# Keeping the first attention group in source order on SyncE and TensorE, and asking for its bulk loads behind the turned probabilities

## The chip, the cores and the metric

One core of one Trainium2 chip runs the whole program. The metric is the device time of one execution in microseconds (us), as the median of several executions. All arithmetic is in float32.

## The reference, cut to what matters

The program is one cross-attention layer and one gated feed-forward layer on 8 sequences of 128 tokens with 512 features, each behind a layer norm and each with its residual. In the attention there are 32 heads of 128 features:

```python
q = rmsnorm(hidden, ln_weight) @ w_q.T        # 8 x 128 x (32*128)
k, v = ctx @ w_k.T, ctx @ w_v.T
score = einsum('bqhd,bkhd->bhqk', q, k) + position_bias
score = softmax(where(mask, score, -inf)); score = where(mask, score, 0)
attn  = einsum('bhqk,bkhd->bqhd', score, v)
x = x + hidden + attn @ w_out.T               # then the gated feed-forward layer
```

## The kernel before

**Tiles and stages.** The 32 heads are handled in eight groups of four (`g` = 0 to 7, `GH` = 4, 512 features wide). All queries are projected first and stored to DRAM (`queries`). Then the attention loop (L1008) runs over the groups, and within a group over the eight sequences `b` (L1030). While the attention of group g runs, the keys and values of group g+1 are projected in the gaps; these projections use two levels of Strassen's seven products, so they consist of many short matmul steps with an addition (VectorE) or a copy (ScalarE) out of PSUM after each. The profile calls their PSUM tiles `mm_k`, `mm_v` (outer products), `m_v` (one outer product carried out as seven inner steps, on only two PSUM banks in turn) and `i_v`, `i_k` (the other inner steps).

**One sequence of a group.** `probabilities` (L547) adds mask and bias on GpSimd (`s<-pb,mneg`), lets TensorE make the four heads' scores (`sc<-k,q`), adds them to `s` on VectorE, takes the row maxima (`nmx`), and on ScalarE takes the exponentials and scales them. `transpose_p` (L582) then turns the probabilities: a VectorE transposition within 32x32 blocks (`tt<-s`), a store to DRAM (`turned<-tt`, 256 KB) and a load in another block order (`pT<-turned`, 256 KB). Both transfers are issued by SyncE, and the load waits until the store has landed. Three sequences later `attend` (L596) multiplies with the values (`av<-pT,v`; in group 0 the values are `v_back`), ScalarE copies the result out (`aT<-av`) and stores it from its own queue (`att<-aT`). Below, "pT(4)" is the turned tile of sequence 4 of group 0, "sc(1,0)" the scores of group 1, sequence 0, and so on.

**What sets the order.** A planner places the instructions of each engine, SyncE's DMA issues among them, from its own estimate of when each can run; it may let one run ahead of what stands before it in the source. `InOrder` (L49) takes that freedom away: an instruction issued through it is pinned behind the instruction that was traced before it on the same engine. Pinned instructions carry the line L60 in the profile, or that of a helper. Each engine then carries out its stream in order, so an instruction that waits holds up what stands behind it.

In group 0 the projection matmuls (`kv_tensor`) are pinned to the end of the group, while the attention's own matmuls (`tensor`: scores and `av`) are pinned for the sequences 0 to 3 only. SyncE's transfers in the loop are not pinned: `load_bias` (L811), `load_kv` (L131), `load_queries` (L816) and the two transfers of `transpose_p`. In the source, the bias of the next group and the weights `wk`, `wv` of the group after it are asked for at the start of each group, and a pair of sequences' queries (512 KB) at every even `b`, two pairs ahead.

**How much projection goes between two sequences** is counted in units: the generator `later_kv` (L644) yields a weight for each step that it issued, and the loop takes steps `while done < due(g, b)` (L992). In group 0 this gives, in source order, after the scores of sequence 6 and `av` of sequence 3: one `mm_v` product and three `m_v` steps; after the scores of sequence 7 and `av` of sequence 4: the other four `m_v` steps and two `i_v` parts.

Of the kernel before, what the change touches and what calls it, by code (L numbers as in the profile page):

```python
# [18 lines left out]
BS = 32  # L19
# [45 lines left out]
def xattn_ffn_kernel(  # L65
# [19 lines left out]
    nc = tc.nc  # L85
# [5 lines left out]
    GH = 4  # L91
# [34 lines left out]
    def load_w(name, src, eng=nc.sync):  # L126
        t = wpool.tile([P, DC, GW], F32, tag="w", name=name)
        eng.dma_start(t, src.rearrange("(c p) n -> p c n", p=P))
        return t

    def load_kv(g):  # L131
        cols = bass.ts(g, GW)
        return load_w(f"wk{g}", wkT[:, cols]), load_w(f"wv{g}", wvT[:, cols])

    def load_q(g):
        return load_w(f"wq{g}", wqT[:, bass.ts(g, GW)], sync)
# [24 lines left out]
    kv_w = {0: (wk0, wv0)}  # L161
    x_in = [acts.tile([P, 2, D], F32, tag="a", name=f"x_{i}") for i in range(B // 2)]
    for b in range(B):
        nc.sync.dma_start(x_in[b // 2][:, b % 2, :], x[b])

    vector, gpsimd, scalar, sync = (
        InOrder(tc, e) for e in (nc.vector, nc.gpsimd, nc.scalar, nc.sync)
    )
# [98 lines left out]
    def turn(eng, sync, name, src, *parts, tags=("tt", 2)):  # L267


        tag, bufs = tags  # L270
        tt = work.tile([P, 4, 4, BS], F32, tag=tag, name=f"tt_{name}", bufs=bufs)
        eng.transpose(tt, src.rearrange("q h j r -> q j h r"))  # L272
        d = next(turns)
        sync.dma_start(
            d.rearrange("i r j n -> (i r) (j n)"), tt.rearrange("p j h c -> p (j h c)")
        )
        def back():
            for to, tiles in parts:
                sync.dma_start(
                    to.rearrange("p i h c -> p i (h c)"),  # L280
                    d[:, :, :, tiles].rearrange("i r j n -> (r j) i n"),
                )
        return back
# [295 lines left out]
        return s  # L579


    def transpose_p(g, b, p):  # L582
        n = f"{g}_{b}"
        pT = work.tile([P, 4, GH, BS], F32, tag="pT", name=f"pT_{n}", bufs=4)
        turn(
            vector, nc.sync, n, p.rearrange("q h (j r) -> q h j r", r=BS), (pT, slice(None))
        )()
        return pT

# [18 lines left out]
    tensor = kv_tensor = nc.tensor  # L608
    pend = []
# [116 lines left out]
    kv_tensor = InOrder(tc, nc.tensor)  # L726
# [46 lines left out]
    for n, _ in enumerate(first_kv()):  # L773
        if n in moments_at:
            pair[moments_at[n]] = norm1_moments(moments_at[n])
        if n in scales_at:
            b = scales_at[n]
# [6 lines left out]
        if n in turns_at:  # L784
            b = turns_at[n]
# [18 lines left out]
    scalar = nc.scalar  # L804
# [3 lines left out]
    vector.tensor_scalar(rs1, mv1[:, :, 1], 1.0, EPS, ALU.mult, ALU.add)  # L808
    InOrder(tc, nc.scalar).activation(rs1, rs1, AF.Sqrt)

    def load_bias(g):  # L811
        pb = work.tile([P, GH, S], F32, tag="pb", name=f"pb{g}")
        nc.sync.dma_start(pb, pbias[g * GH : (g + 1) * GH].rearrange("h q k -> q h k"))
        return pb

    def load_queries(g, i, eng=nc.sync):  # L816
        q = acts.tile([P, GH, 2 * S], F32, tag="a", name=f"q_{g}_{i}")
        eng.dma_start(q, queries[g][:, :, bass.ts(i, 2 * S)])
        return q
# [5 lines left out]
    v = kvs[0][1]  # L825
# [12 lines left out]
    for g in range(NG):  # L838
# [13 lines left out]
        w, heads, name = rows_now, [], f"q{g}"  # L852
# [44 lines left out]
    biases, ahead = {0: load_bias(0)}, {}  # L897
# [8 lines left out]
    gpsimd, vector, kv_tensor = nc.gpsimd, nc.vector, nc.tensor  # L906
# [100 lines left out]
    todo = [(g, i) for g in range(NG) for i in range(B // 2)]  # L1007
    for g in range(NG):  # L1008
        kT, v = kvs.pop(g)
        pb = biases.pop(g)  # L1010
        if g + 1 < NG:
            biases[g + 1] = load_bias(g + 1)
        if g + 2 < NG:
            kv_w[g + 2] = load_kv(g + 2)
        if g == 0:

            ctx_later = Later()
            products = later_kv()
        if g == NG - 2:
            wo_later = Later()  # L1020
            load_wo(2)(wo_later)
        if g == NG - 1:
            tensor, vector = InOrder(tc, nc.tensor), InOrder(tc, nc.vector)
            fetched, next_fetched = {}, {}
            gpsimd, sync, wo_sums = InOrder(tc, nc.gpsimd), InOrder(tc, nc.sync), None
            biased = [masked_bias(gpsimd, g, k, pb) for k in range(2)]

            bulk = InOrder(tc, nc.scalar)
            come[1, 0] = load_att(1, 0, bulk)
        for b in range(B):  # L1030
            if (g, b) == (NG - 2, B - 1):
                come = {(0, 0): load_att(0, 0, nc.sync)}
            if b % 2 == 0:
                qT = ahead.pop((g, b // 2))
                at = todo.index((g, b // 2)) + 2
                if at < len(todo):
                    ahead[todo[at]] = load_queries(*todo[at], nc.sync if g + 1 < NG else bulk)

            if (g, b) == (0, 0):
                tensor = kv_tensor = InOrder(tc, nc.tensor)  # L1040
                vector, scalar, gpsimd = (
                    InOrder(tc, e) for e in (nc.vector, nc.scalar, nc.gpsimd)
                )
                done = next(products) + next(products)
            if g == NG - 1:


                if b + 2 < B:
                    biased.append(masked_bias(gpsimd, g, b + 2, pb))
                for _ in range(2):  # L1050
                    wo_later.next(gpsimd)
                if wo_sums:
                    wo_sums = wo_sums(gpsimd)

                def between():
                    if b == 0:
                        next(products)
                    fetched[b] = att_sums(b, 0, come.pop((b, 0)), vector)

                p = probabilities(g, b, qT, kT, pb, between, biased.pop(0))  # L1060
            elif g == 0 and b < 4:
                def one():
                    nonlocal done
                    done += next(products)

                def one_and_sum():
                    ctx_later.next(vector)
                    one()

                if b == 0:  # L1070
                    biased = [masked_bias(gpsimd, g, k, pb) for k in range(2)]
                biased.append(masked_bias(gpsimd, g, b + 2, pb))
                p = probabilities(g, b, qT, kT, pb, one_and_sum, biased.pop(0), one)
            elif g == 0 and b < 6:
                def three_sums():
                    for _ in range(3):
                        ctx_later.next(vector)

                p = probabilities(g, b, qT, kT, pb, three_sums, biased.pop(0))
            else:  # L1080
                p = probabilities(g, b, qT, kT, pb)
                for _ in range(2):
                    ctx_later.next(vector)
                if g == NG - 2:
                    for _ in range((0, 1, 1, 1, 1, 2, 2, 2)[b]):
                        wo_later.next(InOrder(tc, nc.gpsimd))
            pend.append((g, b, transpose_p(g, b, p), v))
            advance(3)

            if g == NG - 1:  # L1090
                while next(products, None):
                    pass
            else:
                while done < due(g, b):
                    done += next(products)
            if (g, b) == (NG - 2, 2):

                sums.close()
                wos = pools(outp)("wosA", 2, side="right", reuse_waits="tile")
                load_wo(0)(wo_later)  # L1100
                load_wo(1)(wo_later)
            if (g, b) == (0, 3):
                tensor, vector, scalar = nc.tensor, nc.vector, nc.scalar
            if (g, b) == (0, B - 1):
                kv_tensor = nc.tensor
            if (g, b) == (1, B - 1):
                gpsimd = nc.gpsimd
            if g == NG - 1:
                if b == 0:
                    proj.close()  # L1110
                    wos = pools(outp)("wosB", 2, reuse_waits="tile")

                    first_banks = [
                        pl.tile([P, 2, HW], F32, tag=tag, name=f"m{k}_0")
                        for k, (pl, tag) in enumerate(2 * [(ps_mm, "mm")] + 2 * [(ps_b, "i")])
                    ]
                    first_out = out_products(0, list(range(NG)), first_banks, fetched)
                n = (b + 2) % B, (b + 2) // B
                come[n] = load_att(*n, bulk)
                if b < NG - 3:  # L1120
                    wo_sums = load_wo(b + 3)
                if b:
                    next(first_out)
                if b + 2 >= B:
                    next_fetched[n[0]] = att_sums(*n, come.pop(n), gpsimd)


    scalar = InOrder(tc, nc.scalar)
# [15 lines left out]
    vector, gpsimd = nc.vector, nc.gpsimd  # L1144
# [78 lines left out]
    scalar = nc.scalar  # L1223
    for i in range(1, B // 2):
# [10 lines left out]
        tensor = nc.tensor  # L1235
# [105 lines left out]
    vector, t3 = InOrder(tc, nc.vector), h2[0, 1]  # L1341
# [227 lines left out]
    for b in range(HB):  # L1569
# [5 lines left out]
        sa, vector = coming[0], nc.vector  # L1575
# [43 lines left out]
```

## Time and profile before

| | |
|---|---|
| median of 3 runs | 1056.53 us (1056.42 to 1056.57) |
| the profiled execution: its own time | 1060.24 us |
| its span, first to last instruction | 1058.4 us |
| mean granted TensorE clock | 0.998 of full speed |
| TensorE matmuls busy | 1048.6 us (99%) |
| VectorE, GpSimd, ScalarE busy | 723.0, 558.6, 380.7 us |
| moved by DMA | 166.11 MB, 157 GB/s on average |

All start times below are microseconds from the start of the profiled execution's span. Group 0 of the attention begins at about 227 us and the last projection step that is counted to it ends at about 285 us; the products with the values of its last sequences follow by 299 us. A float32 matmul is recorded as two instructions, so "x8" for `sc` or `av` is the four heads of one sequence. An idle time is shown in square brackets with what ended it. A DMA issue is shown with the time that SyncE spent on it; how long the transfer took to land is another view.

### The profile page before, as it was taken

To read this page: it belongs to the slowest core of one execution; us is meant where nothing else is said; L and a number is where in the kernel's file an instruction comes from. 1 tells how busy PE (TensorE), PEld (TensorE's weight loads), DVE (VectorE), ACT (ScalarE), POOL (GpSimd) and SP (SyncE) were. 2 spreads that over 40 slices of the span, in tenths; PEclk is the share of its full clock that TensorE was granted. 3 is DMA by queue.
4 is the path that set the end of the run, shared out by engine and by line. 5 is a ranking of instruction groups with operands and counts; after the bars stand their busy time and mean duration, and the time that the engine had idled before them with its cause. 6 is when DMAs were issued, how large, how long until landed. Compare 5 with 4: busy or idle time off the path is not lost.

```text
span 1058.4 us, 15313 instructions
## 1 busy us (share of the span) xinstructions
PE 1048.6 (99%) x5288; PEld 859.0 (81%) x5288; DVE 723.0 (68%) x1407; ACT 380.7 (36%) x1146; POOL 558.6 (53%) x647
## 2 busy tenths in 40 slices
PE   9999999999899999999999999999999999999998
PEld 5658888876789898988889779998888865667887
DVE  4698888885577777777777645664544247889852
ACT  2541112027555656556555555531000012333100
POOL 6649776808657666656662275570000336997010
PEclk9999999999999999999999999999999999999999
DMA  8443453495555654655656567773442622120011
GB/s 283 149 170 139 155 184 120 147 359 194 176 177 179 191 184 157 208 179 182 199 170 206 179 217 233 237 277 120 164 139 67 196 99 60 41 60 0 1 40 41
DMA packets 125854, 166.11 MB, mean 157 GB/s; under 512 B 15728, under 2 KB 77424, under 8 KB 125776
## 3 DMA queue, kind: packets, MB, share of 16 engines
q1 hardware_dynamic: 111360, 133.92, 38.5%
q10 hardware_dynamic: 12544, 24.38, 6.6%
q0 software_dynamic: 1872, 6.82, 2.1%
q8 instruction: 42, 0.69, 0.3%
q14 instruction: 36, 0.29, 0.1%
HBM read 106.90 MB, written 58.20 MB: 156 GB/s over the span
## 4 chain that ended last, share of the span: by engine, by line
PE 93%; DMA 3%; POOL 2%; DVE 1%; ACT 1%; issue 1%; SPq 0%; ACTq 0%; DVEq 0%; POOLq 0%
PE i_q L60 9%; PE m L967 9%; PE m L60 8%; PE i_v L437 7%; PE d L1525 6%; PE i L1390 6%; PE i_k L404 6%; PE mm_v L522 6%; PE mm_k L501 6%; PE mm_f L1430 5%; PE mm_q L60 4%; PE av L600 4%; PE sc L555 4%; PE mm_k L60 2%; PE mm_v L60 2%; PE m_v L437 2%
## 5 line engine op out<-in xcount | busy, mean ns | idle before, releaser
L60 DVE TENSOR_TENSOR q<-q,i_q 128x512 f32<-128x512 f32 x168 | 94.6, 596 | 20.2 <-PE i_q L60 17.7
L568 ACT ACTIVATE s<-s,nmx 128x128 f32<-128x128 f32 x240 | 93.3, 390 | 28.2 <-DVE nmx L563 20.7
L399 DVE TENSOR_TENSOR v<-v,i_v 128x256 f32<-128x256 f32 (+1 forms) x150 | 76.5, 521 | 33.6 <-PE i_v L437 29.2
L540 POOL TENSOR_TENSOR s<-pb,mneg 128x512 f32<-128x512 f32 x40 | 61.4, 1536 | 66.0 <-DVE tt L272 66.0
L578 ACT ACTIVATE s<-s,ri 128x128 f32<-128x128 f32 x240 | 76.7, 390 | 43.3 <-DVE ri L576 32.1
L399 DVE TENSOR_TENSOR k<-k,i_k 128x512 f32<-128x512 f32 (+1 forms) x105 | 59.3, 587 | 26.2 <-PE i_k L404 25.9
L605 ACT COPY aT<-av 128x512 f32<-128x512 f32 x60 | 35.1, 586 | 114.2 <-PE av L600 98.9
L60 POOL TENSOR_TENSOR s<-pb,mneg 128x512 f32<-128x512 f32 x24 | 36.7, 1535 | 52.7 <-DVE tt L60 36.0
L555 PEld LDWEIGHTS sc<-k,q 128*128 128x128 f32 x416 | 53.9, 192 | 7.0 <-issue 5.3
L555 PE MATMUL sc<-k,q 128*128 128x128 f32 x416 | 55.6, 275 | 0.0
L1164 POOL TENSOR_TENSOR x<-x,u 128x256 f32<-128x256 f32 x4 | 3.0, 754 | 90.9 <-DVE x L1163 90.9
L60 PE MATMUL m<-wo,a 128*128 128x256 f32 x200 | 48.5, 380 | 0.5 <-DMA a<-att 0.5
L967 PE MATMUL m<-wo,a 128*128 128x256 f32 x200 | 48.4, 379 | 0.0
L272 DVE STREAM_TRANSPOSE tt<-s 128x512 f32<-128x512 f32 x52 | 36.8, 709 | 16.3 <-ACT s L578 15.9
L300 DVE TENSOR_TENSOR S_a<-a 128x256 f32<-128x256 f32 x22 | 10.1, 461 | 54.9 <-DMA a<-att 33.3
L600 PE MATMUL av<-pT,v 128*128 128x128 f32 x360 | 47.6, 275 | 0.0
L568 ACT ACTIVATION_READ_ACCUMULATOR s<-s,nmx 128x1 f32 x240 | 44.9, 187 | 0.0
L559 DVE TENSOR_TENSOR s<-sc,s 128x512 f32<-128x512 f32 x52 | 35.3, 679 | 12.5 <-PE sc L555 12.4
L600 PEld LDWEIGHTS av<-pT,v 128*128 128x128 f32 x360 | 43.8, 192 | 0.0
L967 PEld LDWEIGHTS m<-wo,a 128*128 128x128 f32 x200 | 38.0, 190 | 5.2
L60 PEld LDWEIGHTS m<-wo,a 128*128 128x128 f32 x200 | 37.2, 190 | 5.5 <-DMA a<-att 0.9
L60 DVE TENSOR_TENSOR gate<-gate,i 128x512 f32<-128x512 f32 (+1 forms) x60 | 32.9, 592 | 5.3 <-PE i L1390 4.6
(489 smaller groups left out, 2824.9 us busy)
## 6 DMA issues: line engine op xcount, KB each, us to landing
queries<-q SPq DMA_DIRECT2D x32, 512.0 KB, 3.8
turned<-tt SPq DMA_DIRECT2D x64, 256.0 KB, 2.8
pT<-turned SPq DMA_DIRECT2D x64, 256.0 KB, 3.1
att<-aT ACTq DMA_DIRECT2D x64, 256.0 KB, 3.0
q<-queries SPq DMA_DIRECT2D x30, 512.0 KB, 5.1
a<-att SPq DMA_DIRECT2D x23, 512.0 KB, 4.1
wq<-in_wqT_dram SPq DMA_DIRECT2D x8, 1024.0 KB, 6.6
wk<-in_wkT_dram SPq DMA_DIRECT2D x7, 1024.0 KB, 6.1
```

Of the source, the lines that this page charges most:

```text
L60: return self.tc.keep_in_program_order(getattr(self.engine, op)(*args, **kw))
L399: vector.tensor_tensor(to, *(base or [to]), out, ADD)
L404: kv_tensor.matmul(out, a[n][i], b[n][i], start=first, stop=True, skip_group_check=True)
L437: kv_tensor.matmul(out[:, bass.ts(k, S)], b[n][i][:, bass.ts(k, S)], a[n][i], start=first and k == 0, stop=True, skip_group_check=True,)
L501: kv_tensor.matmul(out, w[i][:, c, bass.ts(t, P)], src[i][:, c, :], start=(first and c == 0), stop=(c == HC - 1), skip_group_check=True,)
L522: kv_tensor.matmul(out[:, bass.ts(k, HW)], src[i][:, c, bass.ts(2 * t + k, S)], w[i][:, c, :], start=(first and k == 0 and c == 0), stop=( ...
L555: tensor.matmul(sc[:, j, :], qT[:, j, bass.ts(b % 2, S)], kT[j][:, cols], start=True, stop=True)
L568: scalar.activation(s[:, j, :], s[:, j, :], AF.Exp, bias=nmx[:, j : j + 1], accum_out=sm[:, j : j + 1],)
L578: scalar.mul(s[:, j, :], s[:, j, :], ri[:, j : j + 1])
L600: tensor.matmul(av[:, j, :], v[b // 2][:, b % 2, bass.ts(j, P)], pT[:, :, j, :], start=True, stop=True,)
L967: tensor.matmul(m[n], sa[n][:, c, :], wo_t[g][n][:, c, :], start=(g == order[0] and c == 0 and PRODUCTS.index(n) % 2 == 0), stop=(g == ord ...
L1390: nc.tensor.matmul(out, a[n][k], fine_t[n][k], start=first, stop=True, skip_group_check=True)
```

## The change

The edit does three things in group 0 (one of them, the pinned bias load, in every group).

- SyncE: the two transfers of `transpose_p`, the loads of the bias, and group 0's loads of weights and queries are issued through `InOrder`, so they are pinned in source order.
- The source order of the loads: `wk2` stays at the start of the group; the queries are asked for behind pT(b) of every even `b` instead of ahead of the scores; `wv2` is asked for behind pT(5) instead of at the start of the group. From group 1 on, queries and weights are asked for where they were, and are not pinned; the bias of group 2 is pinned at the start of group 1, behind pT(7).
- TensorE: `tensor` stays pinned to the end of group 0 instead of to sequence 3.

No computation is added or removed.

```diff
-    def load_kv(g):
+    def load_kv(g, kinds="kv", eng=nc.sync):
         cols = bass.ts(g, GW)
-        return load_w(f"wk{g}", wkT[:, cols]), load_w(f"wv{g}", wvT[:, cols])
+        return [load_w(f"w{k}{g}", {"k": wkT, "v": wvT}[k][:, cols], eng) for k in kinds]
...
-    def transpose_p(g, b, p):
+    def transpose_p(g, b, p, sync):
         n = f"{g}_{b}"
         pT = work.tile([P, 4, GH, BS], F32, tag="pT", name=f"pT_{n}", bufs=4)
         turn(
-            vector, nc.sync, n, p.rearrange("q h (j r) -> q h j r", r=BS), (pT, slice(None))
+            vector, sync, n, p.rearrange("q h (j r) -> q h j r", r=BS), (pT, slice(None))
         )()
         return pT
...
-    def load_bias(g):
+    def load_bias(g, eng=nc.sync):
         pb = work.tile([P, GH, S], F32, tag="pb", name=f"pb{g}")
-        nc.sync.dma_start(pb, pbias[g * GH : (g + 1) * GH].rearrange("h q k -> q h k"))
+        eng.dma_start(pb, pbias[g * GH : (g + 1) * GH].rearrange("h q k -> q h k"))
         return pb
...
     for g in range(NG):
         kT, v = kvs.pop(g)
         pb = biases.pop(g)
+        turn_sync = nc.sync if g else InOrder(tc, nc.sync)
         if g + 1 < NG:
-            biases[g + 1] = load_bias(g + 1)
+            biases[g + 1] = load_bias(g + 1, InOrder(tc, nc.sync))
         if g + 2 < NG:
-            kv_w[g + 2] = load_kv(g + 2)
+            kv_w[g + 2] = load_kv(g + 2, "kv" if g else "k", turn_sync)
...
             if b % 2 == 0:
                 qT = ahead.pop((g, b // 2))
                 at = todo.index((g, b // 2)) + 2
-                if at < len(todo):
+                if g and at < len(todo):
                     ahead[todo[at]] = load_queries(*todo[at], nc.sync if g + 1 < NG else bulk)
...
-            pend.append((g, b, transpose_p(g, b, p), v))
+            pend.append((g, b, transpose_p(g, b, p, turn_sync), v))
+            if g == 0 and b % 2 == 0:
+                ahead[todo[b // 2 + 2]] = load_queries(*todo[b // 2 + 2], turn_sync)
+            if (g, b) == (0, 5):
+                kv_w[2] += load_kv(2, "v", turn_sync)
             advance(3)
...
             if (g, b) == (0, 3):
-                tensor, vector, scalar = nc.tensor, nc.vector, nc.scalar
+                vector, scalar = nc.vector, nc.scalar
             if (g, b) == (0, B - 1):
-                kv_tensor = nc.tensor
+                tensor = kv_tensor = nc.tensor
```

## The prediction

> **What bounds the kernel now.** I read the page first. TensorE's matmuls are busy for 1048.6 of 1058.4 us, so the end is TensorE's, and only TensorE's idle time, its clock and its order can move it. Next, who TensorE waited for over the whole span (engine, line, times waited in us: total, count, longest):
>
> ```profile
> PE av L600 <- DMA pT<-turned: 4.1, 2, 3.3
> PE zero L177 <- DVE zeros L174: 1.2, 1, 1.2
> PE mm_k L60 <- ACT k L60: 0.7, 2, 0.4
> PE m L60 <- DMA a<-att: 0.5, 1, 0.5
> ```
>
> Of the waits, 4.1 us are turned probabilities that arrive late, in group 0, which the change touches. TensorE's timeline shows where (start, duration, form, idle before in brackets):
>
> ```profile
> 256.40 1.13 PE L600 MATMUL av<-pT,v_back 128*128 128x128 f32 x8 [0.79 <-DMA pT<-turned]
> ...
> 267.83 1.89 PE L60 MATMUL mm_v<-S_v,ctx_sb 128*128 128x256 f32 x8
> 269.56 0.61 PE L60 MATMUL m_v<-wv,ctx_sb 128*128 128x128 f32 x4
> 270.00 1.06 PE L555 MATMUL sc<-k,q 128*128 128x128 f32 x8
> 274.35 0.91 PE L600 MATMUL av<-pT,v_back 128*128 128x128 f32 x6 [3.28 <-DMA pT<-turned]
> 275.09 0.75 PE L60 MATMUL m_v<-wv,ctx_sb 128*128 128x128 f32 x4
> ```
>
> Two things are to be seen: the waits for pT(1) and pT(4); and that sc(7) and av(4) ran ahead of the second and third `m_v` step, which stand before them in the source. The windows by microsecond (length, busy, granted clock, DMA share, GB/s) show what follows the longer wait:
>
> ```profile
> 272.00:273.00 1.00, 0.00 (x0) 1.00 0.82 213
> 275.00:276.00 1.00, 1.00 (x9) 0.71 0.73 259
> 276.00:277.00 1.00, 1.00 (x7) 0.50 0.14 50
> 277.00:278.00 1.00, 1.00 (x7) 0.50 0.60 170
> 278.00:279.00 1.00, 1.00 (x7) 0.58 0.70 237
> 279.00:280.00 1.00, 1.00 (x12) 1.00 1.00 375
> ```
>
> The clock is halved: 0.29 + 0.50 + 0.50 + 0.42 = 1.7 us of work lost. Why the tiles were late, from SyncE's timeline:
>
> ```profile
> 247.62 0.39 SPq L128 DMA_DIRECT2D wv<-in_wvT_dram  x1
> 248.74 0.37 SPq L279 DMA_DIRECT2D pT<-turned  x1
> ...
> 264.03 0.33 SPq L274 DMA_DIRECT2D turned<-tt  x1
> 267.96 0.37 SPq L813 DMA_DIRECT2D pb<-in_pbias_dram  x1
> 268.44 0.45 SPq L279 DMA_DIRECT2D pT<-turned  x1
> 268.98 0.52 SPq L818 DMA_DIRECT2D q<-queries  x1
> 269.60 0.68 SPq L274 DMA_DIRECT2D turned<-tt  x1
> 270.36 0.52 SPq L818 DMA_DIRECT2D q<-queries  x1
> ```
>
> pT(1) went 1.1 us behind the 1 MB of `wv2` and took 7.5 us to land; pT(4) went among a bias, two loads of queries and another store and took 5.8; undisturbed ones took 2.8 to 3.0.
>
> **What goes.** With `wv2` behind pT(5) nothing large is ahead of pT(1): turned(1), issued at 244.83, took 3.9, so pT(1) lands at about 248.7 + 3 = 251.7, and TensorE wants it at 255.6. The 0.79 goes whole. pT(4): everything on TensorE is 0.79 earlier from here on, so turned(4) goes at 263.2, lands after its 4.0 at 267.2, and pT(4) lands 2.8 (pT(0), which had one load of queries just behind it) to 5.8 later: 270.1 to 273.1. If TensorE does not wait, 3.28 and the clock's 1.7 go too: **0.79 + 3.28 + 1.7 = 5.8 us** is the most that can be had here.
>
> Will the clock's 1.7 be there in the timed runs as well? The row says that one idle time of 3.28 us was followed by 3.4 us at half clock, while 0.79 was followed by none; the timed runs agree within 0.15 us, so they all have it or none has. The Trainium skill ("TensorE: Matmul & The Clock Gate", What's actually happening) says that the clock falls after an idle window of about 3.4 us that runs freely; by its letter 3.28 us need not do it, and the sum would lose its 1.7. I go by the row.
>
> **What strict order on TensorE adds.** The second and third `m_v` steps must now come before sc(7). The second one needs a PSUM bank, and the two banks are those of the last two `mm_v` products; ScalarE copies the last one out here:
>
> ```profile
> 270.58 0.19 ACT L568 ACTIVATION_READ_ACCUMULATOR s<-s,nmx 128x1 f32 x1
> 270.68 0.56 ACT L375 COPY v<-mm_v 128x512 f32<-128x512 f32 x1
> ```
>
> That copy stands behind the four exponentials of sequence 6 and ends at 271.24, while the first `m_v` step ends at 270.00. The planner had filled this hole with sc(7). Both ends move together, so TensorE now waits **1.2 us** for ScalarE (0.6 if the copy is planned ahead of the exponentials, 1.5 with the delays between engines). sc(7), av(4) and all of group 1 are queued behind it. After it come two steps of 0.44 and sc(7) of 0.89, so TensorE wants pT(4) at 271.24 - 0.79 + 1.77 = 272.2: inside the 270.1 to 273.1 above. Only one load and one store stand just behind pT(4) now and no bias ahead of it, so I take 0 of the possible 0 to 0.9.
>
> Then the remaining four `m_v` steps: each must wait for the addition out of its bank (0.42 on VectorE). Before, sc(1,0) and part of an `mm_k` product lay between them; those are still free to float in. Without them the holes are about 1.1 us, with them 0; sc(1,0) needs its queries, now issued at about 267.8 and landing after 5.0 to 6.5 at 272.8 to 274.3, against about 274.1. I take **0.3**.
>
> **What strict order on SyncE adds.** Behind each pT, which waits for its store to land, now stand a bulk load and the next store. SyncE's waits on landed stores were 15.9 us in 4 times between 255 and 285, so this queue does wait. Step by step: queries (1,0) at 267.8, turned(5) at 268.4; 5.7 (a store 1.1 us behind a weight, at 305.62) to 6.5 (at 269.60) later, at 274.1 to 274.9, pT(5), which lands by 279.7 at the latest against av(5) at 284.94 - 4.5 = 280.4. `wv2` follows at 274.6, turned(6) at 275.0; behind the weight it takes 6.1 to 7.5 (turned(2) and pT(1) behind the earlier `wv2`), so pT(6) is issued at 281.1 to 282.5 and lands 2.8 to 4.4 later, at 284 to 287. av(6) stood at 291.09 and would now stand at 286.6: a wait of 0 to 0.4, **0.3** taken. turned(7) and pT(7) follow behind queries (1,1): issue about 283, landing of the store by 289.5, of pT(7) by 292.5, against 298.17 - 4.5 = 293.7. `wv2` itself lands by 283; GpSimd first read it at 289.77, at best 285 now. Bias and `wk2` at the group's start are far from any need: 0. The extra issue times, some 0.4 to 0.5 us each, are in these steps.
>
> The Trainium skill ("DMA: Bandwidth & Descriptors", Anatomy of one DMA) says that a DMA's wait is sat out on the issuing sequencer, which speaks against this change: each moved load delays the next store in series. By that rule alone, with no bulk load able to slip past, the sum is that of the last rival below; no run of the new order has shown it yet.
>
> **Sum.** 5.8 - 1.2 - 0.3 - 0.3 = 4.0, taken as 3.9. Against the profiled execution's own time, 1060.24 - 3.9 = 1056.3; it lies 3.7 above the median, and I carry the difference over unchanged: 1056.53 - 3.9 = **1052.6 us**. With none of the additions it is 1050.7; with 1.5, 0.9, 1.1 and 0.4, which is 3.9, it is 1054.6. That is the likeliest case's own range.
>
> **Rivals.** (1) *The clock's loss is not in the timed runs.* Then 4.1 - 1.8 = 2.3 is left: 1054.2. For it: the dip is seen in one execution. Against: a wait this long was followed at once by the dip.
> (2) *The wait moves to av(6), about even.* If turned(6) takes 7.8 (as `wv2` itself did) and pT(6) 7.5 because queries of group 1, which stay unpinned and went early at 270.36 before, share the transfers, pT(6) lands at 275.0 + 7.8 + 7.5 = 290.3 and av(6) waits 3.7; without a dip 0.3 is gained, 1056.2. For: it is the tightest step. Against: only loads ahead of or around a pT, at 248.74 and 268.44, cost that much.
> (3) *Slower: SyncE's strict chain.* The same place at its worst rows: turned(5) 6.5, turned(6) 8.5 (the longest weight), pT(6) 7.5: 268.4 + 6.5 + 1.0 + 8.5 + 7.5 = 291.9, a wait of 5.3 at av(6), and with it the half clock, 1.7. Net -4.5 + 5.3 + 1.7 = +2.5: 1059.0. It decides from a wait of about 3.3 us on, where the clock falls: pT(6) landing after 289.9.
>
> **Chances.** Forecast 0.63, (1) 0.08, (2) 0.14, (3) 0.15. About 0.2% (2.1 us) is what a measurement of this kernel can tell from no change. Faster: forecast and (1), 0.71, less a little for (1), which lies at that bound: 0.70. Same: 0.14 and that little, 0.15. Slower: 0.15. The range runs from 1050.6 (nothing added) past (2) to 1057.8; what is left out is most of (3) and a little below.
>
> **What the profile will show.** Right: TensorE's waits for pT in total under 1 us; a new wait of 1 to 1.5 us of an `m_v` step for ScalarE's `v` copy, ahead of sc(7); a granted clock of 1.00 in every microsecond from 270 to 290; pT(1) landing in about 3 us; on SyncE wv right behind pT(5). Wrong: any TensorE wait of more than 3 us after 275 (then 2 or 3), a clock below 1 there, or new waits in groups 1 to 6, where TensorE waited for nothing before.

## The result, and the profile after

The forecast was a gain of 3.9 us; the change costs 7.8. The median is **1064.31 us** (1062.68 to 1066.00, 6 runs) against 1056.51 (1056.34 to 1058.93, 6 runs) for the kernel before in the same session: a ratio of 1.0070, 95% interval 1.0058 to 1.0082. The profiled execution after took 1064.04 us with a span of 1062.2.

TensorE's waits between 225 and 300 us (line, times waited in us: total, count, longest). Outside of it stand 1.2 us at the start, as in the kernel before, and four waits of at most 0.4:

```profile
PE mm_v L60 <- ACT v L375: 2.6, 1, 2.6
PE m_v L60 <- ACT v L375: 2.5, 1, 2.5
PE av L60 <- ACT aT L60: 0.5, 1, 0.5
```

No wait for pT is left; in its place TensorE waits twice for ScalarE's copies of value products out of PSUM. TensorE's timeline shows where:

```profile
258.90 1.89 PE L60 MATMUL mm_v<-wv,ctx_sb 128*128 128x256 f32 x8
...
262.41 1.89 PE L60 MATMUL mm_v<-wv,ctx_sb 128*128 128x256 f32 x8
266.94 3.02 PE L60 MATMUL mm_v<-S_v,ctx_sb 128*128 128x256 f32 x8 [2.64 <-ACT v L375]
...
273.92 0.61 PE L60 MATMUL m_v<-wv,ctx_sb 128*128 128x128 f32 x4
277.04 0.71 PE L60 MATMUL m_v<-wv,ctx_sb 128*128 128x128 f32 x4 [2.51 <-ACT v L375]
277.59 0.73 PE L60 MATMUL m_v<-s_v,t_c 128*128 128x128 f32 x4
278.11 1.91 PE L60 MATMUL sc<-k,q 128*128 128x128 f32 x8
279.82 1.79 PE L60 MATMUL av<-pT,v_back 128*128 128x128 f32 x8
```

The second wait is at the place that was forecast (second `m_v` step, ahead of sc(7)) and twice as long; the first, in the middle of the outer products, was not forecast at all. The long durations behind each (3.02 for a product that takes 1.89) are the clock's. The windows by microsecond behind the first wait (length, busy, granted clock, DMA share, GB/s):

```profile
267.00:268.00 1.00, 1.00 (x4) 0.85 0.94 294
268.00:269.00 1.00, 1.00 (x4) 0.50 0.96 302
...
270.00:271.00 1.00, 1.00 (x6) 0.50 0.15 49
271.00:272.00 1.00, 1.00 (x11) 0.94 0.06 12
```

That is 0.15 + 3 x 0.50 + 0.06 = 1.71 us lost. Behind the second wait, from 277 to 282, the clocks 0.97, 0.50, 0.50, 0.50 and 0.82 lose another 1.71.

Why ScalarE was late, from its own timeline. The product that the first copy reads is the one that started at 258.90 and ended at about 261:

```profile
265.92 0.40 ACT L578 ACTIVATE s<-s,ri 128x128 f32<-128x128 f32 x1 [0.24 <-DVE ri L576]
266.23 0.56 ACT L375 COPY v<-mm_v 128x512 f32<-128x512 f32 x1
...
275.24 1.28 ACT L578 ACTIVATE s<-s,ri 128x128 f32<-128x128 f32 x4 [0.24 <-DVE ri L576]
276.42 0.57 ACT L375 COPY v<-mm_v 128x512 f32<-128x512 f32 x1
```

Before, these two copies started at 261.01, in a gap of ScalarE's right behind the product, and at 270.68 (the line stands in the prediction). The first one in the kernel before:

```profile
261.01 0.59 ACT L375 COPY v<-mm_v 128x512 f32<-128x512 f32 x1 [0.46 <-PE mm_v L60]
```

Now the first one stands behind the exponentials and the first scaling of sequence 5, the other behind the four scalings of sequence 6. ScalarE is busy for 36% of the span: it was not too slow, it had been given another order.

SyncE, which the change does pin, did what was forecast:

```profile
263.13 0.33 SPq L60 DMA_DIRECT2D turned<-tt  x1
265.33 0.36 SPq L60 DMA_DIRECT2D pT<-turned  x1
265.74 0.53 SPq L60 DMA_DIRECT2D q<-queries  x1
268.46 0.33 SPq L60 DMA_DIRECT2D turned<-tt  x1
272.73 0.36 SPq L60 DMA_DIRECT2D pT<-turned  x1
273.18 0.46 SPq L60 DMA_DIRECT2D wv<-in_wvT_dram  x1
```

pT(4), issued at 265.33, landed after 2.8 us instead of 5.8, pT(1) after 2.9 instead of 7.5, and `wv2` goes right behind pT(5).

The idle times and the clock in group 0 add up to 2.64 + 2.51 + 0.47 + 3.42 = 9.0 us. (The 0.47 is av(1) waiting for ScalarE's `aT`, where it had waited 0.79 for pT(1).)

### The profile page after: what moved, and what is told of

It reads as the page before. It is cut to its first block, busy times and chain, and to the rows that moved or that the text cites. A ratio compares the mean times of both kernels' runs of the same rounds, so it can differ in the third digit from the quotient of the medians.

```text
span 1062.2 us, 15345 instructions
## 1 busy us (share of the span) xinstructions
PE 1050.7 (99%) x5288; PEld 860.1 (81%) x5288; DVE 723.6 (68%) x1407; ACT 380.8 (36%) x1146; POOL 557.5 (52%) x647
## 4 chain that ended last, share of the span: by engine, by line
PE 94%; DMA 2%; DVE 2%; ACT 1%; issue 1%; POOL 0%; SPq 0%; ACTq 0%; DVEq 0%; POOLq 0%
PE i_q L60 9%; PE m L967 9%; PE m L60 8%; PE i_v L437 7%; PE d L1530 6%; PE i L1395 6%; PE i_k L404 6%; PE mm_v L522 6%; PE mm_k L501 6%; PE mm_f L1435 5%; PE mm_q L60 4%; PE av L600 4%; PE sc L555 4%; PE mm_k L60 2%; PE mm_v L60 2%; PE m_v L437 2%
## 5 line engine op out<-in xcount | busy, mean ns | idle before, releaser
L555 PEld LDWEIGHTS sc<-k,q 128*128 128x128 f32 x384 | 49.4, 192 | 6.4 <-issue 4.8
L555 PE MATMUL sc<-k,q 128*128 128x128 f32 x384 | 51.0, 275 | 0.0
```

The source lines that it names most:

```text
L555: tensor.matmul(sc[:, j, :], qT[:, j, bass.ts(b % 2, S)], kT[j][:, cols], start=True, stop=True)
```

## The experiments

The kernel before ran beside each and had medians of 1057.1 to 1057.4 us. Theory A in the expectations is that the new SyncE order also changed where the planner puts ScalarE's copies. `v_0` to `v_3` below are the four value tiles of group 1 (`v1_0` to `v1_3` in the program) that those copies write.

**1. The kernel before, profiled a second time.**

> The kernel before once more, for a second profile. Its first profiled execution took 1060.24 us, 3.7 more than its median, and I carried that over. If the wait for pT(4) and the half clock behind it (3.28 + 1.7 us) belong to every execution, this profile shows them again at an own time near 1060. If they belong to some executions only, this profile has an own time near 1056.5, a wait for pT of under 2 us in total and no clock below 1 between 270 and 290 us. Then most of the 5.8 us that I counted as the gain was never in the median.

Measured: own time 1057.42 us, span 1055.6, clock 1.000 throughout. TensorE's only wait for pT:

```profile
272.91 0.91 PE L600 MATMUL av<-pT,v_back 128*128 128x128 f32 x6 [2.05 <-DMA pT<-turned]
```

So the first profile showed a costly execution. Such executions occur among the timed runs too: of 52 runs of the kernel before beside the experiments, 14 list a mean granted clock of 0.998 and took 1058.4 to 1060.2 us; the other 38 list 0.999 or 1.000 and took 1055.8 to 1058.5. Here pT(4) took 4.3 us to land, pT(1) 6.0 without a wait, and no clock fell. Group 0 loses 2.05 + 0.47 (`aT`) = 2.5 us, not 5.8. From here to the profile after it is 9.0 - 2.5 = 6.5 us; the two spans differ by 6.6.

**2. TensorE's part alone.**

```diff
             if (g, b) == (0, 3):            # on the kernel before
-                tensor, vector, scalar = nc.tensor, nc.vector, nc.scalar
+                vector, scalar = nc.vector, nc.scalar
             if (g, b) == (0, B - 1):
-                kv_tensor = nc.tensor
+                tensor = kv_tensor = nc.tensor
```

> The kernel before with one part alone: TensorE's scores and av pinned to the end of group 0; SyncE as before. Theory A (ScalarE's copies of mm_v are planned late because tiles of the acts pool get their places in the order of their first use in the source, and the pinned loads of queries (1,0) and (1,1) hold that order up): the copies stay where they were, TensorE waits about 1.2 us for the last one ahead of the second m_v step, the waits for pT shrink because av(4) is asked for 2 us later; 1055.5 to 1058.5. Theory B (TensorE's strict order is what costs the time): two waits of about 2.5 us for ScalarE, each with a half clock; 1062 to 1066.

Measured: 1061.36 us (1061.11 to 1062.56), 1.0038 of before (1.0026 to 1.0051). Both theories' numbers missed. The copies stand in their old places, and the `m_v` step waits as long as the prediction had worked out; the time is lost elsewhere:

```profile
271.09 0.71 PE L60 MATMUL m_v<-wv,ctx_sb 128*128 128x128 f32 x4 [1.12 <-ACT v L375]
279.74 1.20 PE L600 MATMUL av<-pT,v_back 128*128 128x128 f32 x4 [3.46 <-DMA pT<-turned]
```

The second line is av(5), of which the planner put one half ahead of the group's last projection steps, onto a pT(5) that SyncE asks for only at 276.44. A clock loss (0.68 on average from 280 to 284, 1.3 us) follows. So pinning TensorE against the old transfers costs 4.2 us, but not through the late copies.

**3. SyncE's part alone.** The kernel after, with the TensorE lines as before.

> The whole of the change on SyncE, queries included, with TensorE's scores and av free after sequence 3 as before. Theory A: ScalarE's first copy of mm_v stays late (it is a matter of the loads, not of TensorE's pin), but the planner knows that and lets scores run ahead of the mm_v products that wait, so the waits on TensorE are shorter than 2.6 us: 1056 to 1061, below the changed kernel. Theory B (all of the loss is TensorE's pin): the copies are in their old places, 1054 to 1056.

Measured: 1066.68 us (1064.74 to 1068.60), 1.0089 (1.0075 to 1.0102): a miss. The median is above that of the whole change, but the two intervals overlap (1.0058 to 1.0082 there). The six runs fall into two bunches: 1064.7 to 1065.1 at a mean clock of 0.997 to 1.000, and 1068.2 to 1068.6 at 0.995; the profiled execution, 1065.13 at 1.000, is of the first. The four copies start at 266.56, 267.91, 269.27 and 278.50, so they come late without TensorE's pin as well. TensorE, free to run ahead, then waits at more places: 2.4 for `v`, 1.9 for pT, 2.5 and 0.2 for additions on VectorE, 0.9 for `s`.

**4. Queries (1,0) at the same place in SyncE's order, but first used later in the source.** The load moves behind the products that follow sequence 4; everything on SyncE keeps its order.

```diff
-            if g == 0 and b % 2 == 0:
+            if g == 0 and b in (0, 2, 6):
                 ahead[todo[b // 2 + 2]] = load_queries(*todo[b // 2 + 2], turn_sync)
...
+            if (g, b) == (0, 4):       # behind "while done < due(g, b)"
+                ahead[todo[4]] = load_queries(*todo[4], turn_sync)
```

> The changed kernel with one line moved: the load of queries (1,0) is traced behind the projection steps of sequence 4 instead of ahead of them, so that the first value tile's first use comes before it. SyncE's order and TensorE's order stay as in the changed kernel. Theory A: the first copy of mm_v is back ahead of the scaling of sequence 4, the wait of 2.64 us at the mm_v product and the half clock behind it (1.7) go, the wait of 2.5 us at the second m_v step stays: 4.3 us less than the changed kernel, 1059 to 1061. Theory B and a theory of the transfers (C: the strict chain on SyncE makes tiles late): nothing moves, 1063 to 1066.

Measured: 1060.33 us (1058.44 to 1061.42), 1.0024 (1.0014 to 1.0034), as expected. The load goes at 268.55, later than the 265.74 of the kernel after, and yet the first copy is back at 260.79. The wait in `mm_v` is gone, one of 2.98 in `m_v` is left:

```profile
272.93 1.22 PE L60 MATMUL m_v<-wv,ctx_sb 128*128 128x128 f32 x4 [2.98 <-ACT v L375]
```

**5. Queries (1,1) as well.** Experiment 4 with both loads of group 1's queries first used behind the products of their sequence (4 and 6).

> The changed kernel with both loads of queries (1,0) and (1,1) traced behind the projection steps of their sequence, so that the value tiles of that sequence have their first use before them; the loads still stand behind pT(4) and pT(6) on SyncE. Theory A: the copy that the second m_v step waits for is back right behind the exponentials of sequence 6 as well, its wait falls from 2.5 to 3.0 us to about 1.1, and the half clock goes; against the run in which only (1,0) was moved 1.5 to 3.5 us less, so 1057 to 1059. Theory C (the strict chain on SyncE is what made that copy late): the 2.5 to 3.0 us stay, 1060 to 1061.

Measured: 1058.01 us (1057.31 to 1060.36), 1.0006 (0.9998 to 1.0015), as expected. The last copy is back at 270.36, the `m_v` step waits 1.12, and the clock stays at 1.00 in the profiled execution. A wait of 0.81 for ScalarE's `ri`, ahead of av(5), is new. All the rest of the change is in here.

**6. Only queries (1,1) moved.** The kernel after, with the other three loads of group 0's queries unpinned and where they were.

```diff
-                if g and at < len(todo):
+                if (g or b not in (6,)) and at < len(todo):
...
-            if g == 0 and b % 2 == 0:
+            if g == 0 and b in (6,):
```

> The changed kernel with only the last of the four moves of queries, (1,1) behind pT(6); the other three are free as before. Theory A: the first copies are in their old places and no mm_v product waits; the copy ahead of the second m_v step is behind the scaling of sequence 6, so that step alone waits 2.5 to 3 us with half a clock behind it; 1059.5 to 1062. Theory C, that the serial chain counts: with two loads fewer in the pinned chain the wait is near 1.1 us and the time near 1058.9, as with all queries free.

Measured: 1060.13 us (1058.04 to 1062.79), 1.0027 (1.0017 to 1.0038), as expected. Again only the `m_v` wait, again 3.0. The profiled execution is the one of 1058.04. Windows of 2 us behind that wait, of experiment 4 and then of this one:

```profile
272.00:274.00 2.00, 1.07 (x5) 0.63 0.73 267
274.00:276.00 2.00, 2.00 (x11) 0.52 0.28 74
```

```profile
272.00:274.00 2.00, 1.04 (x9) 1.00 0.74 200
274.00:276.00 2.00, 2.00 (x21) 1.00 0.97 347
```

The same wait at the same place halved the clock in one execution and left it alone in the other. The latter is 2.1 us under its own median. The timed runs agree: of the nine of experiment 4, eight list 0.997 or 0.998 (1060.13 to 1061.42 us) and one 1.000 (1058.44); of the seven of this one, six list 0.997 or 0.998 (1059.44 to 1062.79) and one, the profiled one, 1.000.

**7. All queries as before.** The kernel after, with the queries of group 0 unpinned and where they were; all else of the change stays.

> The changed kernel without the move of the queries: their loads are asked for where they were and are free; bias, weights and turned tiles stay pinned as changed, and TensorE too. Theory A: both long waits for ScalarE go, about 1.2 us at the second m_v step stays, no long wait for pT; 1054.5 to 1057.5. Theory B: 1062 to 1066. Theory C: the waits for pT return, 3 us and more in total.

Measured: 1058.91 us (1057.54 to 1062.41), 1.0017 (1.0007 to 1.0027). The copies are back, but the time is 1.4 above what was expected: av(5) waits 1.28 for pT in this order, and the `m_v` step 1.12. Of the 3.4 us to experiment 8 that still leaves about 1 us; small waits in later stages (0.8 for `wo` on GpSimd, 0.8 for `wk`, 0.5 for `wo`'s load) are of that size, but nothing ties them to the change.

**8. The same without TensorE's pin.** Stores, pT, bias, `wk2` and `wv2` pinned on SyncE as in the change, queries and TensorE as before.

> One part of the change alone: on SyncE the turned tiles, the bias and the weights are pinned and asked for as changed, while the queries and TensorE stay as in the kernel before, so TensorE and ScalarE have the order of the kernel before. Theory A, with the gain that the forecast counted: no wait for pT (2.0 to 4.1 us in the two profiles of before), nothing in its place; 1053.5 to 1055.5, which beats both kernels. If the gain was never there: 1056.5 to 1058.

Measured: **1055.53 us** (1054.73 to 1057.16), 0.9983 (0.9974 to 0.9992): 0.03 above the range that was expected with the gain, well below the one without it, and faster than both kernels. No wait for pT; between 240 and 300 TensorE waits once:

```profile
PE av L600 <- ACT aT L60: 0.5, 1, 0.5
```

**9. A buffer of its own for queries (1,0), and the control.** The load stays pinned behind pT(4). To make room, the tile of inner weight rows has one buffer instead of two; the control is the kernel after with that alone.

```diff
-            s = ipool.tile([P, 3, 4, P], F32, tag="rows", name=f"s_{name}", bufs=2)
+            s = ipool.tile([P, 3, 4, P], F32, tag="rows", name=f"s_{name}", bufs=1)
...
-        q = acts.tile([P, GH, 2 * S], F32, tag="a", name=f"q_{g}_{i}")
+        own = (g, i) == (1, 0)
+        q = (qpool if own else acts).tile(
+            [P, GH, 2 * S], F32, tag="q" if own else "a", name=f"q_{g}_{i}"
+        )
...
```

The lines left out open a pool of one buffer, `qpool`, and close it.

> The kernel after with one thing changed in where data lies: queries (1,0) get a buffer of their own instead of a place of the common pool. Their load stays where the change put it, pinned on SyncE behind pT(4), and all other orders in the source stay. To make room the tile of inner weight rows has one buffer instead of two (the control run has that alone). Theory A (the common pool's places are handed out in the order in which the source first uses them, and the late load holds up the value tiles that come after it): the first value copies stand again right behind their products, the first near 261, TensorE's wait of 2.6 us for ScalarE in mm_v and the half clock behind it are gone, the m_v step's wait of 2.5 to 3.0 us stays (that is the fault of queries (1,1)); 3 to 5 us below the control. Rival theory B (the late loads themselves, their transfers or the time that SyncE spends on them, delay the work): the load is as late as before, so the 2.6 us stay and the time is within 1 us of the control's.

> Control for the run above: the kernel after with one buffer instead of two for the tile of inner weight rows, and nothing else. Both theories: group 0 as in the kernel after (waits of about 2.6 us in mm_v and 2.5 us in m_v for ScalarE), and between 0 and 3 us above the kernel after (1064 to 1067) if the second buffer is of use in later groups.

Measured: 1076.05 us (1074.73 to 1078.61) against 1080.20 (1078.35 to 1080.91) for the control, 4.15 apart; their ratios to before are 1.0175 (1.0159 to 1.0191) and 1.0211 (1.0197 to 1.0225). The level of the control was missed by 13 us: with one buffer, two scores of later groups wait 4.8 and 4.6 us for VectorE, in both kernels alike. Group 0 of the control is that of the kernel after (2.63 and 2.51). With a buffer of its own, SyncE's order is unchanged, the load of queries (1,0) goes at 266.45 right behind pT(4), and yet the copies are back:

```profile
260.80 0.58 ACT L375 COPY v<-mm_v 128x512 f32<-128x512 f32 x1 [0.46 <-PE mm_v L60]
265.09 0.56 ACT L375 COPY v<-mm_v 128x512 f32<-128x512 f32 x1
266.74 0.56 ACT L375 COPY v<-mm_v 128x512 f32<-128x512 f32 x1
272.32 0.56 ACT L375 COPY v<-mm_v 128x512 f32<-128x512 f32 x1
```

Only the last one, the fault of queries (1,1), is still late, with its wait of 2.97. So it is not the late transfer that delays the copies, and not SyncE's time: it is that the tile of queries and the value tiles take their places from one pool.

## Why the prediction was wrong

**What happened.** Queries and value tiles are both allocated from the pool `acts` (18 places, one tag). The source uses queries (1,0) for the first time ahead of `v_0`, and queries (1,1) ahead of `v_3`. Once these loads are pinned behind pT(4) and pT(6), the first uses of the value tiles that come after them are planned late too. It is the planned order, and not a wait for the load on the chip: the copy into `v_3`, at 276.42, ran ahead of the load of queries (1,1), at 280.29. The first use of a value tile is ScalarE's copy. Its product sits in one of two PSUM banks, and the TensorE stream, pinned, stops at the next product that needs the bank. Shown: a later first use in the source (experiments 4 and 5) or a pool of its own (9) brings the copies back while SyncE's order stays. Queries (1,0) cost 1064.31 - 1060.33 = 4.0 us (4.15 by experiment 9), queries (1,1) 1060.33 - 1058.01 = 2.3. Apart from the 4.15, these differences are of medians from different sessions; by the ratios to the kernel before of each session they are 4.9 and 1.9. How the planner hands out the places, and which ones the tiles got, was not looked at; only its two inputs were varied.

**Right.** SyncE's steps: pT(1) and pT(4) land in under 3 us, no wait for pT is left, pT(6) comes in time, and `wv2` behind pT(5) harms nothing. The queue does sit out its stores' landing, as the prediction said with the trace (17.3 us in 8 waits ahead of pinned loads between 240 and 300 us, in the kernel after), but nobody waits for it. The `m_v` step's wait of 1.2: 1.12 wherever the copies stand in their old places (2, 5, 7).

**Wrong, in the order of their size** (profile after against experiment 1: +6.5 where -4.0 was forecast, which is 10.5 apart: 7.8 + 3.3 - 0.6 below. The medians moved by +7.8; experiment 1's own time lies 0.9 above the median of the kernel before in the result, and the profile after 0.3 below its median):

- The step that failed most is "Both ends move together" under "What strict order on TensorE adds". It took ScalarE's order for given, since the diff changes nothing of ScalarE's. The bounds of 0.6 to 1.5 came from the copy's place next to the exponentials; a place behind the scalings was not among them (2.51, so 1.3 more), and the copies of the outer products were not looked at (2.64). The half clock behind both adds 3.42, and `aT` 0.47. Together 7.8.
- "What goes", 5.8 us. It was the loss of one costly execution, and experiment 1 has 2.5: 3.3 too much. "The timed runs agree within 0.15 us, so they all have it or none has" was read off three runs and left out the third case, that some have it (14 of 52, by the clocks under experiment 1); the profile's own time, 3.7 us above the median, said that it was not like those three. "I carry the difference over unchanged" put that excess on top of the gain instead of taking it off. The gain that SyncE's part brings without the queries is 1057.06 - 1055.53 = 1.5 us (experiment 8).
- The two terms of 0.3, for the chain of `m_v` steps and for av(6), did not come: 0.6 the other way. (The sum itself came to 4.0 and was taken as 3.9, and the lower end stands as 1050.7 and as 1050.6; 1056.53 - 5.8 is 1050.7. Neither matters here.)

**The rivals.** None was it. The first, that the timed runs lack the clock's loss, was right for most runs of the kernel before, but it kept 4.1 us of waits where experiment 1 has 2.5, and it did not describe the change. The second and third looked for a new wait at av(6), behind SyncE's chain; av(6) waits for nothing. The slower side came from an engine that the change does not name.

**TensorE's pin** has two faces. Against copies in their places it costs 1058.91 - 1055.53 = 3.4 us (7 against 8); against late copies, leaving it out gave a median 2.4 higher (3), which the overlapping intervals leave open. The prediction counted only the first face, at 1.2 + 0.3. Where the one would turn into the other was not tried.

## What to carry to other kernels

When a planner hands out places of a shared pool, moving or pinning one load can move the first use of every tile that the source allocates after it, on whatever engine that use is: list the tiles behind the moved one in its pool, and look for their first writers, before taking the other engines' order for given. A profiled execution whose own time lies above the median of the timed runs can show losses that most of those runs do not have: profile it a second time, or take a gain read from it down by that difference, do not carry it over. Here the 1 MB of `wv2` could stand behind the urgent pT(5) without harm (experiment 8 has no wait for pT); what cost time was the loads whose buffers come from the pool of the value tiles.

## What the runs showed of the hardware

The clock after an idle time of TensorE is not set by the length of that time alone. It was halved for 3 to 3.4 us behind waits of 2.51 and 2.64 us (the kernel after) and 2.98 us (experiment 4), and not behind 2.05, 2.37 and 2.55 (experiments 1 and 3); a wait of 2.97 went without it in experiment 6. The Trainium skill ("TensorE: Matmul & The Clock Gate", What's actually happening) says that the chip looks at windows of about 3.4 us that run freely; that the same wait is punished in one execution and not in another agrees with it, that less than a whole window of idling (2.51 us) suffices does not. Here a wait of 2.5 to 3 us thus cost itself, and in some executions 1.5 to 1.7 us more.
